# A product of u and dt moved from VectorE to GpSimd, and dt summed into SBUF, in a Mamba and mixture-of-experts kernel

## The chip, the cores and the metric

The kernel runs on 1 core of one Trainium2 chip. The metric is device time in microseconds (us). Before the change it takes 1851.69 us, the median of 3 runs (1851.32 to 1852.23).

Engines are named as in the profile: PE is TensorE (matmuls), DVE is VectorE, ACT is ScalarE, POOL is GpSimd, SP is SyncE, which here only issues DMAs. Each engine works through a queue of its own in order; semaphores join the queues.

## The reference

One layer: a Mamba block with a residual and a layernorm, then a mixture of 32 experts (the best 6 for each row) with a shared expert, a residual and a layernorm. Input x is 4096 rows of 256 values, all in float32. The part around the change is the Mamba block (D_INNER 512, D_STATE 16):

```python
xz = x @ W_in.T
x_in, z = jnp.split(xz, 2, axis=-1)
xc = silu(conv(x_in, W_conv) + b_conv)          # depthwise, 4 taps, along the rows
dt = softplus(xc @ W_dt.T + b_dt)
Bm, Cm = xc @ W_B.T, xc @ W_C.T
A = -jnp.exp(A_log)
# for each row l, channel d and state n, with u = xc:
#   h = exp(dt * A) * h + dt * Bm * u
#   y[d] = sum over n of h * Cm
out = (y * silu(z)) @ W_out.T
```

The scan needs dt in two places: alone, in exp(dt * A), and as the product dt * u, which is multiplied by Bm.

## The kernel before

The 4096 rows are cut into 8 chunks of 512. In a chunk the 512 channels stand on 128 partitions in M = 4 groups (m = 0 to 3), with the rows along the free dimension, so that a tile is 128 x 512.

The scan of a chunk is 64 units, one for each of 4 groups m and 16 states n. A unit q takes these steps, issued by one loop in the order in which they stand at the end of this section:

- `exp_at(q + 2)` (L1132, ACT): h = exp(dt * A), from the dt of the chunk into a PSUM bank; 3 such banks.
- `du_at(q + 4)` (L1121, POOL): du = u * B, where u already holds u * dt and B is a row that SP has loaded onto all partitions (bb). du has 6 buffers, bb 3. So POOL works some units ahead of DVE, and a du waits for the scan six units before it, which frees its buffer.
- L1260 (DVE): the scan itself, h = h * previous + du along the 512 rows, in place in PSUM.
- L1267 (DVE): hc = h * C, with the row C from SP's load cb; 4 buffers.
- `keep` (L1159, ACT): the last column of h goes to hlast, for the next chunk.
- `summed` (L1178, PE): hc is transposed and added into y.

All other work is written as generators, and the loop calls `step()` once a unit, which moves each of them to its next `yield`. The order in every queue is fixed by that. Beside the scan of chunk c run

- `front(c + 1, 3)`: the projections, the convolution, u, and dt of the next chunk. The last part of it is what the change touches: dt = relu(v) + ln(1 + exp(-|v|)), of which the first term, with a correction, stands in the SBUF tile `dt` (L956) and the logarithm is written by ACT into a PSUM bank `ln` (L971). Then, one group m at a `yield`, the two are added (L975), u is multiplied by the sum (L976), and the sum goes to SBUF (L977). In chunk 0 this stands ahead of everything; the fronts of chunks 1 to 7 run beside the scans of chunks 0 to 6, and their edited lines fall in units 41 to 51.
- `tail(c - 1)`: gate, output projection, layernorm, router and shared expert of the chunk before. At its end `ranked` starts `copies(c - 1)`, 24 indirect DMAs on POOL's queue that scatter the rows to the experts' lists (xs, L552). They come one a unit, with a unit left out after every third for the earlier chunks, from the second half of a chunk into the first units of the next one. `apart_from` keeps two of these DMAs from following each other with no other POOL work between.
- from chunk 2 on `rest`, the expert tiles: SP loads rows from xs (xt, L614; behind the last scatter of their chunk) and weights (gu, dn), PE, ACT and DVE work on a pair of tiles, and two indirect DMAs on POOL's queue add the results into HBM (acc, L664).

u and dt each have two SBUF buffers, which alternate between chunks; both are cut from the large tile `wall`, so the profile shows them as wall. Matmuls and the softplus take PSUM banks from a ring of 3, counted by `room`, `bank` and `free`.

After the scans the experts' weights have been loaded as a whole (`walls`), the remaining expert tiles run through `through_all`, and `finish` adds the partial results, normalizes and stores.

Of the kernel before, what the change touches and what calls it, by code (L numbers as in the profile page):

```python
# [39 lines left out]
def rounds(k):  # L40
    for _ in range(k):
        yield


def beside(gens, gap):

    gens, going, wait = list(gens), [], 0
    while gens or going:
        going = [g for g in going if alive(g)]
        if gens and wait <= 0:  # L50
            g = gens.pop(0)
            wait = gap
            if alive(g):
                going.append(g)
        wait -= 1
        if gens or going:
            yield
# [3 lines left out]
def kernel(  # L61
# [20 lines left out]
    nc = tc.nc  # L82
# [33 lines left out]
    def blocks(c):  # L116
        return SIZES[c] // P
# [15 lines left out]
    def room():  # L133
        while held[0] >= len(pools):
            yield

    def bank(name):
        held[0] += 1
        turn[0] += 1
        return pools[turn[0] % len(pools)].tile([P, T], F32, tag="mm", name=name)  # L140

    def free():
        held[0] -= 1
# [14 lines left out]
    apart_from = [False]  # L158
# [660 lines left out]
    with ExitStack() as c1:  # L819
# [7 lines left out]
        def load_x(c):  # L827

            t = scratch.rearrange("p m t -> p (m t)")[:, : blocks(c) * D]
            t = t.rearrange("p (b d) -> p b d", d=D)  # L830
            nc.sync.dma_start(
                t, x[AT[c] : AT[c] + SIZES[c], :].rearrange("(b p) d -> p b d", p=P)
            )
            x_in[c] = t
# [32 lines left out]
        def front(c, gap):  # L867

            nb, Tc = blocks(c), SIZES[c]
            xT = xTs[c % 2]  # L870
            xT_of[c] = xT

            def turned(k):
                yield from room()
                pt = bank(f"pxt_{c}_{k}")
                for b in range(nb):
                    nc.tensor.transpose(pt[:, ts(b, P)], x_in[c][:, b, ts(k, P)], ident)
                yield
                nc.scalar.copy(xT[:, k, :Tc], pt[:, :Tc])
                free()  # L880

            yield from beside([turned(k) for k in range(KD)], 1)
            if c:
                last = SIZES[c - 1]
                nc.gpsimd.tensor_copy(xin[:, :, 0:H], xin[:, :, last : last + H])
            yield
            u = us[c % 2][:, :, :Tc]
            u_of[c] = u

            def projected(m):  # L890
                yield from room()
                px = bank(f"px_{c}_{m}")[:, :Tc]
                for k in range(KD):
                    nc.tensor.matmul(
                        px, w_in[:, k, ts(m, P)], xT[:, k, :Tc],
                        start=(k == 0), stop=(k == KD - 1),
                    )
                yield
                nc.scalar.copy(xin[:, m, H : H + Tc], px)
                free()  # L900
                yield
                yield from room()
                pv = bank(f"pv_{c}_{m}")[:, :Tc]
                for k in range(TAPS):
                    nc.tensor.matmul(  # L905
                        pv, taps[:, m, k, :], xin[:, m, k : k + Tc],
                        start=(k == 0), stop=(k == TAPS - 1),
                    )
                yield
                nc.scalar.activation(u[:, m, :], pv, AF.Identity, bias=bcv[:, m : m + 1])  # L910
                free()

            yield from beside([projected(m) for m in range(M)], gap)
            if c:
                yield from gate(c - 1)
            yield
            nc.scalar.activation(u, u, AF.Silu)
            if c:
                nc.scalar.activation(z_of[c - 1], z_of[c - 1], AF.Silu)
                gated.add(c - 1)  # L920
            yield
            yield from room()
            pb = bank(f"pb_{c}")[:, :Tc]
            for k in range(M):
                nc.tensor.matmul(
                    pb[: 2 * NS, :], w_bc[:, k, :], u[:, k, :],
                    start=(k == 0), stop=(k == M - 1),
                )
            yield
            bc = bc_all[: 2 * NS, :Tc]  # L930
            nc.scalar.copy(bc, pb[: 2 * NS, :])
            free()
            dt = dts[c % 2][:, :, :Tc]
            e = scratch[:, :, :Tc]
            dt_of[c] = dt

            def stepped(m):
                yield from room()
                pd = bank(f"pd_{c}_{m}")[:, :Tc]
                for k in range(M):  # L940
                    nc.tensor.matmul(  # L941
                        pd, w_dt[:, k, ts(m, P)], u[:, k, :],
                        start=(k == 0), stop=(k == M - 1),
                    )
                yield
                nc.scalar.activation(dt[:, m, :], pd, AF.Relu, bias=bdt[:, m : m + 1])
                nc.scalar.activation(e[:, m, :], pd, AF.Abs, bias=bdt[:, m : m + 1])
                nc.scalar.activation(e[:, m, :], e[:, m, :], AF.Exp, scale=-1.0)
                nc.scalar.add(pd, e[:, m, :], 1.0)
                yield  # L950
                yield

                nc.vector.scalar_tensor_tensor(
                    pd, pd, -1.0, e[:, m, :], ALU.add, ALU.subtract
                )
                nc.vector.tensor_sub(dt[:, m, :], dt[:, m, :], pd)  # L956
                free()

            yield
            bcd = dram.tile([2 * NS, T], F32, tag="bcd", name=f"bcd_{c}")[:, :Tc]  # L960
            nc.sync.dma_start(bcd, bc)
            bcd_of[c] = bcd
            yield from beside([stepped(m) for m in range(M)], gap)

            for two in range(0, M, 2):
                yield
                while held[0] > len(pools) - 2:
                    yield
                lns = [bank(f"ln_{c}_{m}")[:, :Tc] for m in (two, two + 1)]
                for m, ln in zip((two, two + 1), lns):  # L970
                    nc.scalar.activation(ln, e[:, m, :], AF.Ln, bias=1.0)  # L971
                yield
                for m, ln in zip((two, two + 1), lns):
                    yield
                    nc.vector.tensor_add(ln, ln, dt[:, m, :])  # L975
                    nc.vector.tensor_mul(u[:, m, :], u[:, m, :], ln)  # L976
                    nc.scalar.copy(dt[:, m, :], ln)  # L977
                    free()
            if c + 1 < NC:
                yield from rounds(4)  # L980
                load_x(c + 1)

        def gate(c):

            while c - 1 not in z_done and c:
                yield
            z = z_all[:, : blocks(c)]
            z_of[c] = z

            def projected(b):  # L990
                yield from room()
                pz = bank(f"pz_{c}_{b}")
                for k in range(KD):
                    nc.tensor.matmul(
                        pz, xT_of[c][:, k, ts(b, P)], w_in[:, k, DI:],
                        start=(k == 0), stop=(k == KD - 1),
                    )
                yield
                nc.scalar.copy(z[:, b, :], pz)
                free()  # L1000

            yield from beside([projected(b) for b in range(blocks(c))], 2)
# [73 lines left out]
        def state(q):  # L1076

            c, g, s, i = units[q]
            return (2 * s + i, 2 * g, 2) if short(c) else (s, 2 * g + i, 1)
# [115 lines left out]
        for _ in range(8):  # L1195
            for b in range(NB):
                nc.tensor.transpose(pt[:, ts(b, P)], ident, ident)
        free()
        first = front(0, 1)
        blanks = blanked(0, bound(0), 0)  # L1200
        threads.append(first)
# [21 lines left out]
        for q, (c, g, s, i) in enumerate(units):  # L1223
# [35 lines left out]
            n, m, k = state(q)  # L1259
# [158 lines left out]
```

## Time and profile before

| what | us |
|---|---|
| median of 3 runs | 1851.69 |
| profiled execution | 1859.8 |
| its span | 1857.9 |
| first scan starts, last scan starts | 72.0, 1507.0 |
| scan L1260 x512, DVE | 657.1 |
| hc L1267 x512, DVE | 354.3 |
| du L1121 x512, POOL | 694.9 |
| row scatter xs L552 x192, POOL | 192.3 |
| add to acc L664 x224, POOL | 352.3 |
| sum, product, copy (L975, L976 DVE, L977 ACT), median of one | 0.690, 0.686, 0.586 |

Length of each chunk's scan, from its first scan to that of the next chunk, and DVE's idle time in it, by the starts of L1260 and the gaps of DVE in the trace:

| chunk | 0 | 1 | 2 | 3 | 4 | 5 | 6 | 7 |
|---|---|---|---|---|---|---|---|---|
| length | 141.4 | 171.0 | 171.2 | 185.2 | 196.5 | 192.4 | 191.2 | 188.0 |
| DVE idle | 8.7 | 13.8 | 15.2 | 17.7 | 30.1 | 23.2 | 23.0 | 30.2 |

How to read the profile's rows: a group of instructions has its line, engine, operation, output and inputs, shape and count, then its busy time in us and the mean of one in ns, then the idle time of the engine just before them with what ended most of it ("417.5 <-DVE h L1260 216.8": of 417.5 us idle, 216.8 ended when that instruction released it). A timeline row is start, duration, engine, line, operation, and in brackets the idle time before it. A row of a table of windows has, for each engine, busy us and number of instructions, then the TensorE clock that was granted, the DMA engines' busy share and GB/s. On POOL an indirect DMA's row overlaps the start of the next instruction.

### The profile page before, as it was taken

The numbers are of one execution on the slowest core, as the hardware profiler recorded it, in microseconds if no ns is written. First come the engines' busy times: TensorE is split into PE (matmuls) and PEld (weight loads), VectorE is DVE, ScalarE is ACT, GpSimd is POOL, SyncE is SP. The second block draws the span as 40 slices with busy tenths as digits, with TensorE's granted clock in tenths as the row PEclk, the third lists the DMA queues.
The fourth block names the chain that finished last, engine by engine and source line by source line (L and its number), as shares of the span: only waits on it lengthen the run. The fifth ranks groups of instructions, "written<-read, shape, count | busy, mean of one in ns | idle before, by whom it ended". The sixth has DMA issues, their size and how long they took to land. (4 is left out here: it accounts for less than half of the span.)

```text
span 1857.9 us, 24110 instructions
## 1 busy us (share of the span) xinstructions
PE 1359.2 (73%) x6208; PEld 944.8 (51%) x6208; DVE 1399.4 (75%) x2328; ACT 990.9 (53%) x2131; POOL 1216.3 (65%) x961
## 2 busy tenths in 40 slices
PE   8585696588669866986699668967775668699940
PEld 4242453355345545653566456645654566477730
DVE  1689989998998899779987998799979854122217
ACT  3676464547445755475557465756552333355533
POOL 0455644774585569665886599658956874878863
PEclk9796697779769887988989888988886987799975
DMA  8443692673469667875989589858998996599879
GB/s 238 136 126 102 219 307 77 164 212 123 94 192 257 166 160 177 251 206 126 258 215 263 131 234 245 236 139 214 271 257 236 260 268 100 123 145 144 144 131 306
DMA packets 318121, 355.40 MB, mean 191 GB/s; under 512 B 65056, under 2 KB 245024, under 8 KB 317984
## 3 DMA queue, kind: packets, MB, share of 16 engines
q1 hardware_dynamic: 274400, 296.02, 56.7%
q0 software_dynamic: 41472, 57.80, 17.3%
q8 instruction: 51, 0.84, 0.2%
q14 instruction: 86, 0.70, 0.1%
q10 hardware_dynamic: 2112, 0.05, 0.1%
HBM read 244.97 MB, written 108.77 MB: 190 GB/s over the span
## 5 line engine op out<-in xcount | busy, mean ns | idle before, releaser
L1121 POOL TENSOR_TENSOR du<-wall,bb 128x512 f32<-128x512 f32 x512 | 694.9, 1390 | 417.5 <-DVE h L1260 216.8
L1260 DVE TENSOR_TENSOR_SCAN h<-h,hlast,du 128x512 f32<-128x512 f32 x512 | 657.1, 1283 | 52.2 <-ACT hlast L1159 27.3
L1178 PE MATMUL y<-ident,hc 128*128 128x128 f32 x2048 | 345.2, 311 | 124.0 <-DVE hc L1267 104.0
L1132 ACT ACTIVATE h<-wall,aneg 128x512 f32<-128x512 f32 x512 | 353.7, 692 | 95.0 <-DVE hc L1267 80.4
L1267 DVE TENSOR_TENSOR hc<-h,cb 128x512 f32<-128x512 f32 x512 | 354.3, 692 | 58.6 <-DMA cb<-bcd 14.2
L1178 PEld LDWEIGHTS y<-ident,hc 128*128 128x128 f32 x2048 | 278.6, 162 | 233.9 <-DVE hc L1267 136.3
L552 POOL DMA_INDIRECT xs<-row,at x192 | 192.3, 1001 | 72.5 <-issue 39.2
L664 POOL DMA_INDIRECT acc<-ytl,no x112 | 174.8, 1561 | 59.4 <-issue 32.9
L664 POOL DMA_INDIRECT acc<-yt,no x112 | 177.5, 1585 | 53.2 <-ACT yt L658 28.7
L1159 ACT COPY hlast<-h 128x1 f32<-128x1 f32 x448 | 70.9, 158 | 260.7 <-DVE hc L1267 260.4
L1310 DVE SCALAR_TENSOR_TENSOR gt<-gt,pg 128x256 f32<-128x256 f32 x56 | 23.6, 421 | 175.5 <-ACT gt L1308 175.5
L682 PE MATMUL pg<-xsT,gu 128*128 128x128 f32 x896 | 123.8, 297 | 31.5 <-ACT xsT L644 25.4
L682 PEld LDWEIGHTS pg<-xsT,gu 128*128 128x128 f32 x896 | 118.0, 210 | 46.8 <-ACT xsT L644 29.5
L700 PE MATMUL po<-dn,hm 128*128 128x256 f32 x224 | 75.6, 469 | 83.5 <-DVE hm L694 35.6
L941 PE MATMUL pd<-wall 128*128 128x512 f32 x256 | 127.9, 649 | 9.5 <-DVE key L469 4.2
L905 PE MATMUL pv<-wall 128*128 128x512 f32 x256 | 117.4, 602 | 5.9 <-ACT hlast L1159 3.2
L1301 PE MATMUL pg<-wall,xsT 128*128 x448 | 113.0, 398 | 1.0 <-ACT xsT L644 1.0
L700 PEld LDWEIGHTS po<-dn,hm 128*128 128x128 f32 x224 | 46.9, 228 | 102.2 <-DVE hm L694 33.5
L641 PE MATMUL pt<-ident,xt 128*128 128x128 f32 x448 | 76.7, 298 | 24.1 <-DMA xt<-xs 21.2
L1301 PEld LDWEIGHTS pg<-wall,xsT 128*128 128x128 f32 x448 | 85.1, 200 | 12.3 <-ACT xsT L644 2.1
L941 PEld LDWEIGHTS pd<-wall 128*128 128x128 f32 x256 | 51.6, 211 | 66.8 <-issue 60.6
L641 PEld LDWEIGHTS pt<-ident,xt 128*128 128x128 f32 x448 | 61.0, 155 | 41.9 <-issue 25.3
(192 smaller groups left out, 1929.0 us busy)
## 6 DMA issues: line engine op xcount, KB each, us to landing
bb<-bcd SPq DMA_DIRECT2D x256, 256.0 KB
cb<-bcd SPq DMA_DIRECT2D x256, 256.0 KB
xs<-blank SPq DMA_DIRECT2D x55, 578.0 KB
xt<-xs SPq DMA_DIRECT2D x224, 128.5 KB
gu<-in_gate_up_t_dram SPq DMA_DIRECT2D x112, 256.0 KB
dn<-in_down_t_dram SPq DMA_DIRECT2D x112, 128.0 KB
wall<-acc SPq DMA_DIRECT2D x24, 512.0 KB
acc<-blank SPq DMA_DIRECT2D x16, 512.0 KB
```

The source lines that it names most:

```text
L552: i = nc.gpsimd.indirect_dma_start(out=xs, out_offset=bass.IndirectOffsetOnAxis(ap=at[:, b, k : k + 1], axis=0), in_=row[:, b, :], in_offs ...
L641: nc.tensor.transpose(pt4[:, i, k, :], xt[:, i, ts(k, P)], ident)
L664: a = nc.gpsimd.indirect_dma_start(out=acc[(j + i) % LANES], out_offset=bass.IndirectOffsetOnAxis(ap=no[:, i : i + 1], axis=0), in_=yt[:, ...
L682: nc.tensor.matmul(pg[:, h, i, :], gu[i][:, k, ts(h, P)], xT[:, i, k, :], start=(k == 0), stop=(k == KD - 1),)
L700: nc.tensor.matmul(po[:, i, :], hm[:, i, :], dn[i], start=True, stop=True)
L941: nc.tensor.matmul(pd, w_dt[:, k, ts(m, P)], u[:, k, :], start=(k == 0), stop=(k == M - 1),)
L1121: nc.gpsimd.tensor_mul(parts(q, du), u, row_for(q, 0))
L1132: nc.scalar.activation(h[:, ts(i, Tc)], dt_of[c][:, m + i, :], AF.Exp, scale=aneg[:, m + i, n : n + 1],)
L1178: nc.tensor.matmul(y_of[c, g][b // 2][:, b % 2, ts(m + j - 2 * g, P)], hc[:, ts(j * nb + b, P)], ident, start=(opens and j == 0 and b % 2 ...
L1260: nc.vector.tensor_tensor_scan(h, h, du_of.pop(q), hlast[:, n, m : m + 1], ALU.mult, ALU.add)
L1267: nc.vector.tensor_mul(parts(q, hc), parts(q, h), row_for(q, 1))
L1301: nc.tensor.matmul(pg[:, i].rearrange("p h t -> p (h t)"), xT[:, i, k, :], w, start=(k == 0), stop=(k == KD - 1),)
```

## The change

In the last part of `front`, for each group m: the sum of the logarithm and dt goes to the SBUF tile `dt` and no longer back to the PSUM bank; the copy from that bank to `dt` on ACT is gone; the bank is given back after the sum; the product of u and dt is issued on POOL, with dt from SBUF, and `apart_from` is cleared ahead of it, as it is ahead of a du.

```diff
                 for m, ln in zip((two, two + 1), lns):
                     yield
-                    nc.vector.tensor_add(ln, ln, dt[:, m, :])
-                    nc.vector.tensor_mul(u[:, m, :], u[:, m, :], ln)
-                    nc.scalar.copy(dt[:, m, :], ln)
+                    nc.vector.tensor_add(dt[:, m, :], dt[:, m, :], ln)
                     free()
+                    apart_from[0] = False
+                    nc.gpsimd.tensor_mul(u[:, m, :], u[:, m, :], dt[:, m, :])
```

In the compiled program DVE has 32 instructions less, ACT 32 less, POOL 32 more; all others stand in their queues in the order they had. On POOL the product of a group comes right behind the du that its unit issues, and ahead of the xs scatter, where the unit has one. In the changed kernel's listing the product has line L978 (L976 before).

## The prediction

> **What bounds the kernel now.** I read the busy shares first, then the two groups that make up the scan, then the rows of the three edited lines, then the waits and the timeline of GpSimd (POOL) against VectorE (DVE).
>
> ```profile
> PE 1359.2 (73%) x6208; PEld 944.8 (51%) x6208; DVE 1399.4 (75%) x2328; ACT 990.9 (53%) x2131; POOL 1216.3 (65%) x961
> ...
> L1121 POOL TENSOR_TENSOR du<-wall,bb 128x512 f32<-128x512 f32 x512 | 694.9, 1390 | 417.5 <-DVE h L1260 216.8
> L1260 DVE TENSOR_TENSOR_SCAN h<-h,hlast,du 128x512 f32<-128x512 f32 x512 | 657.1, 1283 | 52.2 <-ACT hlast L1159 27.3
> ```
>
> The shares are means over unlike stages. The eight chunks of 64 units (one scan, L1260, and one product, L1267, each) run from 72 to 1508 us, and there DVE is busy almost throughout: of 1436 us it idles some 160. POOL feeds it one du (L1121) per unit and is on the whole ahead: half of POOL's idle time before du ends with a scan, which gives back one of six du buffers. But POOL also issues the row scatters (xs, L552, 24 a chunk) and, from chunk 3 on, the adds to acc (L664), and these come late in a chunk. Two answers side by side, chunk 0 (72 to 164 us) and the late part of chunk 3 (700 to 752 us), give the busy times of PE, PEld, DVE, ACT and POOL and then clock and DMA:
>
> ```profile
> 72.00:164.00 92.00, 72.67 (x268) 38.67 (x268) 85.60 (x95) 61.59 (x121) 52.58 (x43) 0.87 0.41 123
> ...
> 700.00:752.00 52.00, 36.53 (x184) 28.74 (x184) 48.23 (x59) 26.77 (x64) 47.69 (x39) 0.70 0.72 185
> ...
> 1094.00:1145.00 51.00, 37.55 (x222) 31.71 (x223) 47.22 (x59) 28.57 (x70) 46.48 (x39) 0.83 0.88 246
> ```
>
> In chunk 0 POOL is idle 39 of 92 us; late in chunk 3 it is busy 92%, and the rest is 2.1 + 1.4 us of issue gaps and 0.6 us of waits for ACT. DVE and POOL are both full there. I subtracted the end of each du from the start of its scan: the lead is 8 to 15 us around the edited lines in every chunk, and then it falls: to 7.6 us at the end of chunks 1 and 2, to 0.0 at the end of chunk 3, to 0.0, 1.8 and 0.5 us soon after the ends of chunks 4, 5 and 6. So at four chunk ends POOL, not DVE, sets the pace.
>
> **The edited lines.**
>
> ```profile
> L975 DVE TENSOR_TENSOR ln<-ln,wall x32: 689/690/700, 57.1 to 1290.5; 128x512 f32<-128x512 f32 x32
> ...
> L976 DVE TENSOR_TENSOR wall<-wall,ln x32: 686/686/689, 58.0 to 1291.2; 128x512 f32<-128x512 f32 x32
> ...
> L977 ACT COPY wall<-ln x32: 579/586/588, 58.7 to 1292.0; 128x512 f32<-128x512 f32 x32
> ```
>
> DVE loses 32 products of 0.69 us, 22 us in all, 2.8 us a chunk in chunks 0 to 6 (the last chunk has no front beside it). ACT loses 32 copies of 0.59 us; ACT is 53% busy and each copy was mostly a wait for DVE (51.1 us in 30 waits), so I count nothing for it: the cover is ACT's idle time, and uncovered it would be a gain of 28 x 0.59 = 16.5 us at most. The add keeps its place; its output goes to SBUF, and L956, which adds PSUM to SBUF with an SBUF output, takes 687 ns: no change. The ln bank is free one copy earlier; PE's waits that such a copy ends are 2.1 us at the worst line, and PE is not the bound here, so nothing. The queues of PE and SP hold the same instructions in the same order; no DMA is added or moved. No clearing of apart_from matters: each unit's du has cleared it just before.
>
> POOL gains 32 products of the shape of du, at its median, 1.28 us (minimum 1.25, maximum 1.90; the longer ones follow an acc add, and the add's extra then moves from the du to the product). Four a chunk make 5.1 us of POOL time. Each product also waits for DVE's add of the same unit. Queued behind it are the next xs scatter and the du of four to five units ahead, and with a lead of 8 to 15 us POOL gets to the product before DVE gets to the add. So the lead itself is lost there.
>
> **Chunk 3 worked out.** The four adds of chunk 3 stand at 689.3, 693.2, 703.0 and 706.9. This is POOL, then DVE:
>
> ```profile
> 700.83 1.84 POOL L1121 TENSOR_TENSOR du<-wall,bb 128x512 f32<-128x512 f32 x1
> 702.83 1.02 POOL L552 DMA_INDIRECT xs<-row,at  x1 [0.16 <-issue]
> 703.89 1.27 POOL L1121 TENSOR_TENSOR du<-wall,bb 128x512 f32<-128x512 f32 x1
> 705.33 1.01 POOL L552 DMA_INDIRECT xs<-row,at  x1 [0.17 <-issue]
> ...
> 702.99 0.69 DVE L975 TENSOR_TENSOR ln<-ln,wall 128x512 f32<-128x512 f32 x1
> 703.71 0.69 DVE L976 TENSOR_TENSOR wall<-wall,ln 128x512 f32<-128x512 f32 x1
> ...
> 738.91 1.29 DVE L1260 TENSOR_TENSOR_SCAN h<-h,hlast,du 128x512 f32<-128x512 f32 x1 [0.96 <-POOL du L1121]
> ...
> 748.92 1.00 POOL L552 DMA_INDIRECT xs<-row,at  x1 [0.17 <-issue]
> ...
> 752.45 0.34 SPq L614 DMA_DIRECT2D xt<-xs  x1
> ```
>
> The first product stands before a du that now starts at 687.85. The add ends at 689.96, the product at 691.3: that du is 3.5 us late. The second stands before the xs of 689.25; POOL comes at 692.6, the add (one L976 earlier) ends at 693.15, the product at 694.45: 5.2 us late. A wait of 1.2 us at 693.96 takes 1.2 back. Third and fourth find POOL late and the add done, and cost 1.3 each: 6.3 us of backlog at the xs of 705.33. From there to 752 POOL has 0.6 us of waits to lose it in. The lead at the end of the chunk was 0.0 (the scan of 738.91 already waited for du), so, with half of those 0.6 us made good, the scans end 6.0 us later than now, although DVE has 2.8 us less to do. Late next are the last xs (748.92), the tile load that waits for its landing (xt at 752.45), and the bb and cb loads in SP's queue behind it. Now POOL idles 8.4 us before 767.1 for such a bb, and DVE waits for cb; both move along, so I take nothing back.
>
> The same arithmetic for the other chunks (backlog after the fourth product; lead left; half of the waits in which POOL can catch up): chunk 4: 2.9 - 0.0 - 0.9 = +2.0; chunk 5: 4.9 - 1.8 - 0.7 = +2.4; chunk 6: 6.5 - 0.5 - 0.6 = +5.4. In chunks 1 and 2 the backlog is 3.6 and 5.7 us against a lead of 7.6 us and 1 to 3 us of waits: no stall, each gains 2.8, and so does chunk 0, where POOL idles 0.7 us a unit. Later scatters at the start of chunk 3 give back some 0.5. At the start of the kernel four products of 1.28 follow an add that ends at 57.8: the first du goes from 62.7 to about 63.1, and the loads in SP's queue behind the du buffers, which start the scan, with it: +0.4.
>
> Sum: 0.4 - 3 x 2.8 + 0.5 + 6.0 + 2.0 + 2.4 + 5.4 = +8.3 us. The stretch behind the scan (1508 to 1858) starts from its end, and moves along. The profiled execution took 1859.8 us (span 1857.9), 0.4% above the median of 1851.7; the difference is added to the median: 1860.
>
> **Does POOL slow DVE?** In the trace the 512 scans take 1278 to 1293 ns and the 512 hc 690 to 694, whether POOL works or not, so I charge DVE nothing. The Trainium skill (Perfetto Trace Analysis, Optimizing Scalar/DVE Operations) warns that moving work between GpSimd and VectorE might not help, as they share an SBUF read port; its page SBUF — State Buffer (Who interferes with whom) limits this to VectorE instructions with two SBUF inputs or in a two-port mode. The trace shows no such loss for scans and products that read one operand from PSUM. By the warning taken at its worst each of 28 products would hold DVE for its 1.28 us, 36 us more.
>
> **The rivals.**
> *DVE stays the bound.* POOL's backlog is absorbed (in waits at the chunk starts, where POOL idles up to 16.8 us in eight units of chunk 4 and 14.3 in chunk 7), and the 28 products off DVE count in full: 28 x 0.69 = 19 us, 1832; with a third of it lost, 1838; with half of the four backlogs coming through (8 us more than that first value), 1840. For it: DVE is the busier engine, and its 30 us of idle time in chunk 4 and in chunk 7 are mostly waits on tiles and loads, which might not move along. Against it: the four zero leads. It decides for faster where the scans of chunks 3 to 6 end less than 1.9 us late each: 4 x 1.9 is the 7.5 us that chunks 0 to 2 gain with the two small losses taken off.
> *The backlog is never made good.* Chunks 1 and 2 stall as well, and late scatters hold tile loads behind which bb and cb wait: 3.6 + 5.7 + 6.3 + 2.9 + 4.9 + 6.5 = 30 us less chunk 0's 2.8: +27, 1879. Against it: 12.3 us of POOL idle time in units 16 to 23 of chunk 2.
> *They cancel.* Gains in chunks 0 to 2 and losses in 3 to 6 differ by under 3.7 us.
>
> **How the numbers follow.** My forecast (slower, 1856 to 1870) has 0.50, the unabsorbed backlog 0.14, cancelling 0.12, DVE as the bound 0.24. A measurement of this kernel can tell about 0.2%, 3.7 us, from no change. Bounds of the sum: product at 1.25 to 1.90 us (28 x 0.62, up to 17 us more); ACT's copies worth up to 16.5 us; waits absorbed wholly or not at all. The range goes from 1840, the rival with half of the backlogs, to 1875, short of the worst; under 0.2 lies outside. Forecast alone: 1856 to 1870.
>
> **What would show it.** In the changed profile: the new product's row on POOL x32 near 1.28 us, with its waits ended by DVE's add, longest in chunks 0 to 3; DVE idle before scans, ended by POOL du, up from 5.6 us to some 20, at units 58 to 63 and the first units of the next chunk; chunks 0 to 2 shorter by 2.8 us each, chunks 3 and 6 longer by 5 to 6. I am wrong if that wait stays under 10 us, if the product costs DVE time, or if the last xs of a chunk is not later.

## The result, and the profile after

| | before | changed |
|---|---|---|
| median, us (6 runs each, same chip) | 1852.97 (1851.32 to 1857.29) | 1870.88 (1868.75 to 1875.42) |
| ratio, 95% interval | 1 | 1.0096 [1.0079, 1.0112] |
| profiled execution, its span | 1859.8, 1857.9 | 1869.1, 1867.4 |
| last scan starts | 1507.0 | 1525.6 |
| from there to the end of the span | 350.9 | 341.8 |

The change costs 17.9 us. The two profiled spans differ by only 9.5 us, because the stretch behind the scan is 9.1 us shorter in this profile. Whether the change shortens it isn't settled: it takes 348.9 us in a second profile of before, 343.5 and 348.6 us in two more of the changed kernel. The start of the last scan is 18.6 us later, close to what the medians say.

The page of the changed kernel, busy shares and the two groups of the scan:

```profile
PE 1356.4 (73%) x6208; PEld 939.2 (50%) x6208; DVE 1384.2 (74%) x2296; ACT 974.9 (52%) x2099; POOL 1254.7 (67%) x993
...
L1121 POOL TENSOR_TENSOR du<-wall,bb 128x512 f32<-128x512 f32 x512 | 695.4, 1392 | 315.6 <-DVE h L1260 196.2
L1260 DVE TENSOR_TENSOR_SCAN h<-h,hlast,du 128x512 f32<-128x512 f32 x512 | 657.2, 1284 | 78.6 <-ACT hlast L1159 36.7
```

The relief is there (DVE has 32 instructions fewer and 15 us less to do; the products alone took 22, but some short rows take longer here), and so is the load (POOL has 38 us more to do). No scan became slower: 1284 ns as against 1283. But POOL waits 100 us less before its du, and DVE waits 26 us more before its scans. The answer on the scan's line says for whom:

```profile
L1260 DVE TENSOR_TENSOR_SCAN h<-h,hlast,du x512: 1277/1283/1293, 73.6 to 1525.6; 128x512 f32<-128x512 f32 x171
...
  ACT hlast L1159: 36.7, 15
  ACT h L1132: 22.3, 17
  POOL du L1121: 18.9, 23
```

Before, these were 27.3, 18.4 and 5.6 us. Waits for du grow by 13 us, and waits for ACT, which was given less work, by another 13. The two windows late in chunks 3 and 6 (PE, PEld, DVE, ACT, POOL, clock, DMA, GB/s) show the same from the other side:

```profile
700.00:752.00 52.00, 28.58 (x153) 22.11 (x153) 39.31 (x48) 20.25 (x50) 47.94 (x39) 0.69 0.61 165
1094.00:1145.00 51.00, 34.02 (x209) 29.86 (x207) 43.91 (x55) 28.62 (x69) 46.99 (x39) 0.85 0.89 241
```

POOL is as full as before (47.7 and 46.5 then). DVE falls from 48.2 to 39.3 us and ACT from 26.8 to 20.3 in the first: the other engines wait for a queue that was already full. The added rows themselves (the sum on DVE, then the product on POOL):

```profile
L975 DVE TENSOR_TENSOR wall<-wall,ln x32: 675/678/687, 57.2 to 1302.8; 128x512 f32<-128x512 f32 x32
```

```profile
L978 POOL TENSOR_TENSOR wall<-wall x32: 1259/1268/1859, 58.1 to 1308.9; 128x512 f32<-128x512 f32 x32
...
  DVE wall L975: 78.3, 9
```

Of the 78.3 us, 56.2 are POOL's idle time before the first product of the kernel, ahead of the scans, where nothing else is to be done. Beside the scans the products wait 22.1 us, 4.2 to 4.8 at the first of chunks 0, 1 and 2, 2.2 at that of chunk 3 and 3.7 at that of chunk 6.

Where the time goes, by chunk. The table takes the start of unit 36's scan of a chunk (ahead of the edited lines) to the same unit of the next chunk, and compares means: two profiles of before (that of the prediction and e1_control) and three of the changed kernel (this one, e5_changed, e12_changed_again).

| stretch, from the middle of chunk | 0 | 1 | 2 | 3 | 4 | 5 | 6 | 7 to last scan |
|---|---|---|---|---|---|---|---|---|
| before, mean | 167.7 | 171.2 | 180.2 | 195.5 | 194.5 | 193.5 | 186.1 | 72.6 |
| changed, mean | 165.0 | 170.8 | 178.4 | 200.7 | 197.2 | 201.1 | 192.4 | 70.7 |
| difference | -2.7 | -0.4 | -1.8 | +5.2 | +2.7 | +7.6 | +6.3 | -1.9 |
| forecast | -2.8 | -2.8 | -2.3 | +6.0 | +2.0 | +2.4 | +5.4 | 0 |

With +1.2 us ahead of chunk 0's middle the last scan starts 16.4 us later in the mean. A warning on such a table: the two profiles of the same kernel before differ by 0.1 us or less in the three stretches up to the middle of chunk 3, but by 1.1, 4.3, 1.6, 2.0 and 1.9 us in the stretches behind it. One profile's cell from chunk 3 on says little by itself; what all the profiles of one kind share says more.

The POOL timeline late in chunk 3, the changed kernel:

```profile
686.80 1.27 POOL L978 TENSOR_TENSOR wall<-wall 128x512 f32<-128x512 f32 x1 [2.23 <-DVE wall L975]
688.03 1.28 POOL L1121 TENSOR_TENSOR du<-wall,bb 128x512 f32<-128x512 f32 x1
690.08 1.27 POOL L978 TENSOR_TENSOR wall<-wall 128x512 f32<-128x512 f32 x1 [0.77 <-DVE wall L975]
691.50 1.01 POOL L552 DMA_INDIRECT xs<-row,at  x1 [0.16 <-issue]
...
703.15 1.86 POOL L978 TENSOR_TENSOR wall<-wall 128x512 f32<-128x512 f32 x1
705.17 1.02 POOL L552 DMA_INDIRECT xs<-row,at  x1 [0.17 <-issue]
...
707.46 1.27 POOL L978 TENSOR_TENSOR wall<-wall 128x512 f32<-128x512 f32 x1
...
724.35 1.59 POOL L664 DMA_INDIRECT acc<-yt,no  x1 [0.17 <-issue]
...
752.23 1.00 POOL L552 DMA_INDIRECT xs<-row,at  x1 [0.17 <-issue]
```

The first two products wait for the sum, the other two come late and find it done, as forecast. The last scatter goes out at 752.23 instead of 748.92. One more row counts here: the add to acc at 724.35, the second of the two that read one yt buffer, was issued at 720.84 before. What it held up stands on ACT, first before, then changed:

```profile
726.20 0.84 ACT L658 ACTIVATE yt<-po,wt 128x256 f32<-128x256 f32 x2 [4.90 <-DMA acc<-yt,no]
```

```profile
729.27 0.84 ACT L658 ACTIVATE yt<-po,wt 128x256 f32<-128x256 f32 x2 [13.95 <-DMA acc<-yt,no]
730.00 0.16 ACT L1159 COPY hlast<-h 128x1 f32<-128x1 f32 x1
```

L658 scales an expert's output into yt, of which there are two buffers; a buffer comes free when both adds that read it have landed. ACT waited 9 us longer for one: it came 6.0 us earlier (715.32 instead of 721.30) and got it 3.1 us later. Behind it in ACT's queue stand the scan's own hlast copy and exp. So DVE met its two waits in this order:

```profile
730.99 1.29 DVE L1260 TENSOR_TENSOR_SCAN h<-h,hlast,du 128x512 f32<-128x512 f32 x1 [8.31 <-ACT hlast L1159]
...
742.22 1.29 DVE L1260 TENSOR_TENSOR_SCAN h<-h,hlast,du 128x512 f32<-128x512 f32 x1 [1.21 <-POOL du L1121]
```

Before, these scans started at 727.92 and 738.91 with 1.02 and 0.96 us of idle time. DVE had been up to 6 us ahead of its old times in chunk 3 and ends it 3.3 us behind. The wait for ACT used up what it was ahead; the wait that comes last is for du. The late scatter is then felt on SP's queue, where the tile load xt went out at 752.45:

```profile
756.09 0.34 SPq L614 DMA_DIRECT2D xt<-xs  x1
```

### The profile page after: what moved, and what is told of

It is laid out like the page before. It is cut to its first block, busy times and chain, and to the rows that moved or that the text cites. A ratio compares the mean times of both kernels' runs of the same rounds, so it can differ in the third digit from the quotient of the medians.

```text
span 1867.4 us, 24107 instructions
## 1 busy us (share of the span) xinstructions
PE 1356.4 (73%) x6208; PEld 939.2 (50%) x6208; DVE 1384.2 (74%) x2296; ACT 974.9 (52%) x2099; POOL 1254.7 (67%) x993
## 5 line engine op out<-in xcount | busy, mean ns | idle before, releaser
L1260 DVE TENSOR_TENSOR_SCAN h<-h,hlast,du 128x512 f32<-128x512 f32 x512 | 657.2, 1284 | 78.6 <-ACT hlast L1159 36.7
L1178 PE MATMUL y<-ident,hc 128*128 128x128 f32 x2048 | 341.1, 308 | 131.8 <-DVE hc L1267 111.0
L1178 PEld LDWEIGHTS y<-ident,hc 128*128 128x128 f32 x2048 | 273.5, 160 | 241.8 <-DVE hc L1267 144.6
L941 PE MATMUL pd<-wall 128*128 128x512 f32 x256 | 131.8, 665 | 9.2 <-DVE key L469 3.4
L905 PE MATMUL pv<-wall 128*128 128x512 f32 x256 | 121.4, 619 | 11.9 <-ACT wall L899 6.5
L700 PEld LDWEIGHTS po<-dn,hm 128*128 128x128 f32 x224 | 46.0, 224 | 107.1 <-DVE hm L694 34.6
L978 POOL TENSOR_TENSOR wall<-wall 128x512 f32<-128x512 f32 x32 | 42.7, 1339 | 78.4 <-DVE wall L975 78.3
```

Of the source, the lines that this page charges most:

```text
L700: nc.tensor.matmul(po[:, i, :], hm[:, i, :], dn[i], start=True, stop=True)
L905: nc.tensor.matmul(pv, taps[:, m, k, :], xin[:, m, k : k + Tc], start=(k == 0), stop=(k == TAPS - 1),)
L941: nc.tensor.matmul(pd, w_dt[:, k, ts(m, P)], u[:, k, :], start=(k == 0), stop=(k == M - 1),)
L1178: nc.tensor.matmul(y_of[c, g][b // 2][:, b % 2, ts(m + j - 2 * g, P)], hc[:, ts(j * nb + b, P)], ident, start=(opens and j == 0 and b % 2 ...
L1260: nc.vector.tensor_tensor_scan(h, h, du_of.pop(q), hlast[:, n, m : m + 1], ALU.mult, ALU.add)
```

## The experiments

They ran in three groups, each on one chip, with the kernel before measured beside them: 1864.76 us in the first group (e1 to e4), 1858.16 in the second (e5 to e8), 1863.22 in the third (e9 to e12). Ratios are to the kernel before of the same group. The stretches of the table above, as differences from the mean of the two profiles of before, one profile each:

| stretch, from the middle of chunk | 0 | 1 | 2 | 3 | 4 | 5 | 6 | 7 | ratio |
|---|---|---|---|---|---|---|---|---|---|
| e2 sum only | +0.6 | +2.0 | +3.4 | +1.2 | +2.4 | +0.8 | +0.5 | +0.8 | 1.0030 |
| e3 no product | -3.0 | -2.5 | -2.6 | +0.3 | +0.4 | +4.0 | +0.8 | +0.6 | 0.9964 |
| e6 early fronts only | -2.4 | -1.4 | -2.7 | -0.4 | -2.4 | -0.8 | -1.8 | -2.1 | 0.9963 |
| e7 POOL's load alone | +1.1 | -0.4 | +0.1 | +6.6 | +3.7 | +10.3 | +6.7 | -1.0 | 1.0189 |
| e8 product deferred | -2.1 | -0.9 | -2.9 | +3.6 | +2.3 | +8.2 | +2.9 | -1.1 | 1.0080 |
| e9 changed, history on ACT | -3.1 | -1.1 | -3.6 | +4.9 | +0.3 | -0.2 | +7.1 | +1.6 | 1.0022 |
| e10 before, history on ACT | +1.3 | -0.1 | -0.1 | -0.6 | -3.7 | -1.7 | +0.1 | -0.5 | 0.9966 |

**e1_control**: the kernel before once more, for a second profile.

> The kernel before once more, for a second profile. The changed kernel's last scan ends 18.6 us later than in the profile of before, but its span is only 9.5 us longer: the stretch behind the scans took 348.9 us in that profile and 339.8 us in the changed one. If that stretch is 9 us longer by chance in the one profile, the last scan here ends again near 1509 us and the stretch behind it is near 340 us. If the change shortens that stretch, it is again near 349 us.

One execution took 1869.85 us; its last scan starts at 1519.0, 12.0 us later than in the first profile, nearly all of it behind the middle of chunk 3, and the stretch from there on takes 348.9 us. So neither of the two outcomes came as written: the stretch is as long as in the first profile, but the last scan doesn't come back near 1509. That is the spread against which single profiles are to be read.

**e2_sum_only**: the sum goes to SBUF and ACT's copy is gone, but the product stays on DVE.

```diff
-nc.vector.tensor_add(ln, ln, dt[:, m, :])
-nc.vector.tensor_mul(u[:, m, :], u[:, m, :], ln)
-nc.scalar.copy(dt[:, m, :], ln)
+nc.vector.tensor_add(dt[:, m, :], dt[:, m, :], ln)
 free()
+nc.vector.tensor_mul(u[:, m, :], u[:, m, :], dt[:, m, :])
```

> The sum goes to SBUF and the copy on ACT is gone, but the product stays on DVE, now with both operands from SBUF. If GpSimd's work is what costs time, this is the time of before, 1849 to 1856. If the sum to SBUF is what costs, it is near 1871. If ACT's 28 copies were on the path, it is down to 1837. If a product with two SBUF operands and GpSimd hold each other up, the product's row is clearly above 687 ns.

1870.25 us, ratio 1.0030 [1.0012, 1.0048]: a small loss instead of nothing. The answer on the product's line and one of its rows, with POOL's du, in the timelines of DVE and POOL, show why:

```profile
L977 DVE TENSOR_TENSOR wall<-wall x32: 691/692/2934, 57.4 to 1307.1; 128x512 f32<-128x512 f32 x32
```

```profile
1282.08 2.93 DVE L977 TENSOR_TENSOR wall<-wall 128x512 f32<-128x512 f32 x1
```

```profile
1281.95 2.51 POOL L1120 TENSOR_TENSOR du<-wall,bb 128x512 f32<-128x512 f32 x2
```

The product now reads both operands from SBUF, and 12 of the 32 take over 0.8 us; this one spans both du that POOL runs meanwhile. All 32 take 34.6 us instead of 22.0. The run therefore doesn't price the sum's new place cleanly: 12.6 us of DVE time came with it. It does bound it: most of the loss of the change isn't in this half.

**e3_no_product**: as the changed kernel, without the product u * dt anywhere.

```diff
 nc.vector.tensor_add(dt[:, m, :], dt[:, m, :], ln)
 free()
-apart_from[0] = False
-nc.gpsimd.tensor_mul(u[:, m, :], u[:, m, :], dt[:, m, :])
```

> As the changed kernel, but the product of u and dt is left out everywhere, so DVE is relieved and GpSimd gets nothing (the output differs). If GpSimd sets the chunk ends from chunk 3 on, DVE's 2.8 us a chunk count in chunks 0 to 2 and little behind that: 1839 to 1846. If DVE bounds every chunk, 28 x 0.69 = 19 us are gained: 1832 to 1835.

1858.09 us, ratio 0.9964 [0.9948, 0.9979], -6.7 us. DVE is relieved of as much as in the change and POOL is charged nothing, and yet only chunks 0 to 2 gain (-3.0, -2.5, -2.6); from chunk 3 on the 11 us taken off DVE are not seen. If DVE set the pace throughout, some 19 us would have come out. So behind chunk 2 DVE's relief is worth next to nothing in this kernel; the last group below shows a place where it is lost again.

**e4_both**: as e2, and besides a product dt * dt on POOL into a spare tile.

```diff
 nc.vector.tensor_mul(u[:, m, :], u[:, m, :], dt[:, m, :])
+apart_from[0] = False
+nc.gpsimd.tensor_mul(spare, dt[:, m, :], dt[:, m, :])
```

> DVE keeps its product, and GpSimd gets one of the same shape as well (dt by dt, into a tile that nothing reads), at the place of the changed kernel's. If GpSimd's load and wait cost by themselves, the chunks 3 to 6 lose as in the changed kernel and chunks 0 to 2 gain nothing: 1873 to 1885, above the changed kernel by what DVE's relief is worth beside them. If the backlog is mostly absorbed and the loss comes from something in the product itself (u written by GpSimd, read later), 1852 to 1860.

1890.68 us, ratio 1.0140 [1.0113, 1.0166]. It is mixed with what e2 found (its DVE products take up to 3.5 us, and POOL's some 1.5 instead of 1.04 where the two overlap), so it says only that POOL's load costs well over what DVE's product does. e7 repeats it with DVE's product left as it was.

**e5_changed**: the changed kernel in the second group.

> The changed kernel again, beside the three others of this call: 1.006 to 1.013 of before.

1872.58 us, ratio 1.0086 [1.0055, 1.0117].

**e6_early**: the changed lines for the fronts of chunks 1 to 3 alone, which run beside the scans of chunks 0 to 2; elsewhere the old ones.

```diff
+if 0 < c < 4:
+    nc.vector.tensor_add(dt[:, m, :], dt[:, m, :], ln)
+    free()
+    apart_from[0] = False
+    nc.gpsimd.tensor_mul(u[:, m, :], u[:, m, :], dt[:, m, :])
+    continue
 nc.vector.tensor_add(ln, ln, dt[:, m, :])
```

> The change in the fronts of chunks 1 to 3 alone, which run beside the scans of chunks 0 to 2; the fronts of chunk 0 and of chunks 4 to 7 are as before. If GpSimd has room in chunks 0 to 2 and none from chunk 3 on, the gain there stays and the loss is gone: 0.9965 to 0.999 of before, 2 to 6 us faster than before and some 20 us faster than the changed kernel. If every product on GpSimd costs alike, 12 of the 28 cost 12/28 of the change's loss: 1.003 to 1.005.

1850.94 us, ratio 0.9963 [0.9947, 0.9979]: faster than before. The three early stretches keep their gain (-2.4, -1.4, -2.7) and no later one is longer. The loss belongs to the products of chunks 3 to 6.

**e7_pool_alone**: the three old lines stay, and POOL gets dt * dt into a spare tile besides.

```diff
 nc.scalar.copy(dt[:, m, :], ln)
 free()
+apart_from[0] = False
+nc.gpsimd.tensor_mul(spare, dt[:, m, :], dt[:, m, :])
```

> The kernel before, with its three lines untouched, and in addition a product on GpSimd (dt by dt, into a tile that nothing reads) behind ACT's copy, at the place of the changed kernel's. No two-operand product from SBUF runs on DVE here. If GpSimd's load and its wait are the whole cost, it is the changed kernel's loss plus DVE's relief: 1.010 to 1.016. If the loss comes from u being written by GpSimd, 1.000 to 1.003.

1893.42 us, ratio 1.0189 [1.0157, 1.0220]: more than expected of it, although this product is shorter than the real one. The answer on its line:

```profile
L981 POOL TENSOR_TENSOR spare<-wall x32: 1033/1039/1616, 59.7 to 1324.4; 128x512 f32<-128x512 f32 x32
...
  ACT wall L978: 63.6, 9
  ACT hlast L1162: 37.8, 16
```

It waits for ACT's copy, often until the hlast copy behind it. Without the 57.8 us ahead of the first product, that is 43.6 us of waits, against 22.1 in the changed kernel. So it doesn't measure the changed kernel's product exactly. The pattern is what counts: chunks 0 to 2 bear the load for nothing (+1.1, -0.4, +0.1), chunks 3 to 6 pay 27 us for it.

**e8_deferred**: each product five units later, when its sum is long done.

```diff
-apart_from[0] = False
-nc.gpsimd.tensor_mul(u[:, m, :], u[:, m, :], dt[:, m, :])
+if c:
+    threads.append(later(u[:, m, :], dt[:, m, :]))
+else:
+    nc.gpsimd.tensor_mul(u[:, m, :], u[:, m, :], dt[:, m, :])
...
+def later(u, dt):
+    yield from rounds(5)
+    apart_from[0] = False
+    nc.gpsimd.tensor_mul(u, u, dt)
```

> The changed kernel with each product of the fronts of chunks 1 to 7 issued five units later, when DVE's sum is long done; the number of products is the same. If GpSimd's 5.1 us of work a chunk is the cost, the product's 78 us of waits vanish and the time hardly does: 1.005 to 1.009. If the wait for the sum is the cost, 0.995 to 1.002.

1871.6 us, ratio 1.0080 [1.0048, 1.0111], the same as e5 within the intervals. The 28 products beside the scans now wait for nothing (their answer names no idle time), and take 1278 ns. So the 22 us of waits for the sum don't show as a cost, and the work does; the two intervals together leave room for some 8 us either way.

The last group follows a row that the prediction didn't have. On POOL's queue, behind these scatters and adds, also stands L885, a copy of 128x12 values: the history of the convolution for the next front. ACT's L899 writes into the same tile and waits for it. ACT's timeline early in chunk 6, before and changed:

```profile
1143.42 0.59 ACT L899 COPY wall<-px 128x512 f32<-128x512 f32 x1 [2.88 <-POOL wall L885]
...
1147.80 0.69 ACT L910 ACTIVATE wall<-pv,bcv 128x512 f32<-128x512 f32 x1 [1.40 <-PE pv L905]
```

```profile
1153.40 0.59 ACT L899 COPY wall<-px 128x512 f32<-128x512 f32 x1 [5.80 <-POOL wall L885]
...
1160.68 0.69 ACT L910 ACTIVATE wall<-pv,bcv 128x512 f32<-128x512 f32 x1 [4.31 <-PE pv L905]
```

Both waits are 2.9 us longer, and exp and hlast stand behind them. But the product isn't needed for that. These are the same two rows of e3, which has no product on POOL:

```profile
1138.83 0.59 ACT L899 COPY wall<-px 128x512 f32<-128x512 f32 x1 [5.80 <-POOL wall L885]
...
1146.11 0.69 ACT L910 ACTIVATE wall<-pv,bcv 128x512 f32<-128x512 f32 x1 [4.31 <-PE pv L905]
```

The edit for e9 (on the changed kernel), e10 (on before) and e11 (on e6) is the same:

```diff
-nc.gpsimd.tensor_copy(xin[:, :, 0:H], xin[:, :, last : last + H])
+nc.scalar.copy(xin[:, :, 0:H], xin[:, :, last : last + H])
```

**e9_changed_hist**

> The changed kernel, with the copy of the last three columns of xin (L885) on ScalarE's queue instead of GpSimd's, where it stands behind the late scatters and adds. In the changed kernel's trace ScalarE's copy L899 waits for it 13.2 us in three waits, 8.4 us in the trace of before, and the time lost between chunks 5 and 6 exceeds GpSimd's backlog by about 4 us from there on. If that wait is this part of the loss, 3 to 8 us less than the changed kernel of this call. If the tile loads behind the last scatter set the time anyway, within 2 us of it.

1866.14 us, ratio 1.0022 [1.0007, 1.0037].

**e10_before_hist**

> The kernel before with the same move of L885 alone. Its waits are 8.4 us in three, in chunks in which GpSimd has little or no lead. If they are on the path there too, 0.996 to 0.999 of before; if GpSimd's late scatters set the time anyway, 0.999 to 1.001.

1856.1 us, ratio 0.9966 [0.9952, 0.9980].

**e11_early_hist**

> The change in the fronts of chunks 1 to 3 alone, and L885 on ScalarE's queue. If the two gains add up, 0.993 to 0.996 of before; if the second is nothing, that of the first alone, 0.996 to 0.997.

1851.05 us, ratio 0.9940 [0.9920, 0.9960]: the best of all versions here.

**e12_changed_again**: the changed kernel in the third group.

> The changed kernel beside the one with L885 moved, on the same chip: 1.007 to 1.011 of before.

1878.42 us, ratio 1.0078 [1.0050, 1.0106]. The four together: the copy's move is worth 0.34% without the change and 0.56% with it; the change costs 0.78% with the copy on POOL and 0.56% with it on ACT. By the times alone the difference of 0.2% (some 4 us) is within the intervals. The stretches are clearer: the one from the middle of chunk 5 takes 200.6 to 201.7 us in all four profiles of kernels with the late products in full and the copy on POOL (changed three times, e8), 192.7 and 194.3 before, and 193.3 in e9. The loss lies in a short part of it, from the scan of unit 5 of chunk 6, about when ACT begins to wait for L885, to that of unit 26. Against the mean of before, this part is 5.9 to 7.2 us longer in the three changed profiles, 6.8 in e8, 7.3 in e7 and 7.1 in e3, and within 0.1 of it in e2, e6 and e9. So the loss goes with L885 on POOL's queue (its absence rests on e9's one profile), but either DVE's relief (e3) or POOL's load (e7) comes with it; what sets it off stays open. In e9 ACT's answer on L899 has no wait for L885 left:

```profile
L899 ACT COPY wall<-px x32: 577/587/589, 9.8 to 1169.7; 128x512 f32<-128x512 f32 x32
...
  PE px L894: 17.1, 24
```

## Why the prediction was right, and where its size was off

The direction, the place and the range were right: slower, from chunk 3 on, inside 1840 to 1875. The size was +8.3 us against a measured +17.9 (+14.4 and +15.2 in the second and third group), and 1870.9 lies just above the narrower forecast of 1856 to 1870.

*Product on POOL, 1.28 us.* Median 1268 ns, mean 1339, the longest 1859: right. The waits for the sum are longest in chunks 0 to 2, as forecast, but the 3.7 us in chunk 6 exceed those of chunk 3. e8 shows that without them the loss is the same within the intervals. The scans' waits for du, forecast at some 20 us, are 18.9.

*POOL is full from the edited lines of chunks 3 to 6 on.* Right. From the middle of each of these chunks to its last scatter, the changed kernel falls behind by 5.4, 3.0, 3.8 and 6.8 us in the means of the table, against forecast backlogs of 6.3, 2.9, 4.9 and 6.5. e6, e7 and e3 show the three sides of it: no late product, no loss; the load alone loses there and, but for 4 us ahead of chunk 0's middle, nowhere else; relief of DVE alone gains nothing there.

*From backlog to time.* Here it failed, in one term. The prediction took back lead and half of POOL's waits, 0.3 to 2.5 us a chunk. In chunk 3 that made +6.0 (measured +5.2), in chunk 6 +5.4 (+6.3) and in chunk 4 +2.0 (+2.7); there the time lost is about POOL's backlog as measured. But in the stretch from the middle of chunk 5 it made +2.4, and +7.6 came, more than POOL's backlog of 3.8. That term alone is 5.2 of the 8.1 us by which the last scan's mean start missed the forecast. What it lacked: "late next" named the xs scatters, the tile loads and the loads in SP's queue, but not L885, which stands on POOL's queue behind them and holds ACT. Up to unit 5 of chunk 6 the three changed profiles are only 0.7 to 1.2 us behind the mean of before; the 21 units behind ACT's wait for L885 add 5.9 to 7.2. With L885 away from POOL they add nothing (e9), e9 stands at +1.5 us to e10 in the stretch, and the whole change costs 0.56%, about 10 us: close to the forecast of 8.3. That is one profile, and by the times the difference from 0.78% isn't clear of the intervals. Nor is it the product alone that brings this loss: e3 without it gains 3.1 us up to unit 5 and then loses 7.1. The profile of before had shown the row: 8.4 us of waits of L899 for L885.

*ACT as cover.* The copies were counted at nothing because ACT is 53% busy. No run shows a gain from them, though none takes them out alone. But ACT isn't free of POOL. It waits on POOL's queue twice, at L899 as above and at L658, where the wait for the landing of an earlier add was 8.7 us in the first profile of before, 1.3 in the control, 10.7 in e10 and 10.6 in e6, and 20.4 to 24.6 in the five profiles with all products on POOL. Half of DVE's added waits in the changed profile, 13 of 26 us, come through ACT (hlast, exp) and not through du. The prediction had the scans wait for du alone. Not all of it is cost: late in chunk 3 the wait for ACT is the longer one, but du's comes last. Whether more yt buffers would cut the wait at L658 wasn't tried.

*Chunks 0 to 2, -2.8 us each.* Together -4.9 where -7.9 was forecast (its 0.5 us for late scatters in it); e3 without any product gains 8.1, e6 with the products 6.5. So the relief of DVE was sized right and part of it is lost again when POOL carries the product, though POOL has idle time there. The lead at the end of chunks 1 and 2 falls from 7.6 us to 2.3 and 1.9, so it was nearly used up as reckoned. Which waits took the rest isn't settled.

*The start, +0.4.* +1.1 in the mean; all the profiles of all kernels lie between -0.7 and +3.9 us of the first profile's first scan, so it can't be told from nothing.

*DVE isn't slowed by POOL.* Right for the rows that count: scans 1284 ns, the sum (one operand from PSUM) 678 ns. Eight short rows of the tails (L185) take 7.5 us together instead of 4.3, but 7.0 in e3 too, so that isn't the product's doing.

*The rivals.* DVE as the bound falls with e3. The prediction held four zero leads against it, but two of the four were 1.8 and 0.5 us by its own reading, and its 1840 takes half of the four terms as they come through (15.8 us), not of the backlogs (20.6). The backlog that is never made good (+27) was half right: in the stretches from chunks 3 to 6 21.8 us come through, of measured backlogs of 19.0 and what L885 adds, but chunks 1 and 2 together absorbed most of theirs. Cancelling is out.

## What to carry to other kernels

Before work is moved to an engine that looks idle on average, look at the stage where its queue is full, and list everything that stands in that queue behind the new work, small copies and indirect DMAs too, with who waits for each: a wait can reach the bottleneck through a third engine, and here a relief of the bottleneck alone (e3) ran into the same row. The same edit may gain in one stage and lose in another; the split by stage (e6) kept the gain. A 0.2 us copy on a crowded in-order queue cost more than it would on an engine with gaps, and moving it (e10, e11) paid by itself.

## What the runs showed of the hardware

A DVE product with both operands in SBUF takes 0.69 us alone, but up to 2.93 us while POOL works on tensors (e2: the 12 of 32 over 0.8 us overlap POOL's tensor work by 0.33 us or more, the others by 0.24 at most), and POOL's product beside it 1.48 to 1.55 us instead of 1.04 (e4). With one operand in PSUM 32 of 32 took 686 to 689 ns. The Trainium skill (SBUF — State Buffer, Who interferes with whom) says that a VectorE instruction with two SBUF inputs contends with a GpSimd instruction that reads SBUF; these runs agree.

On POOL a 128x512 product takes 1.27 us with two different operands and 1.04 with the same operand twice (e7).
